# Second graph layer: one-hot sums in three bf16 parts in place of fp32 products

## The chip, the cores and the metric

The kernel runs on one core of a Trainium2 chip, in one launch. The metric is the device time of one execution in microseconds. Eleven executions of the kernel before took 3299.36 to 3309.21 us, with a median of 3303.67 us. The engines are named as the profile names them: PE (TensorE, the matrix engine; PEld is its weight load), DVE (VectorE), ACT (ScalarE), POOL (GpSimd) and SP (SyncE).

## What is computed

The reference is two rounds of a graph network with a feed-forward block after each. There are 6250 nodes with 256 features and 106,250 edges, sorted by destination. The change lies in the graph step of the second round. It projects every node, squares, sums the squares over a node's incoming edges with the weight of each edge, takes the root, and projects again:

```python
h = jax.nn.relu(x @ Wp.T + bp)            # 6250 x 128
hp = h ** MU                              # MU = 2
msgs = edge_vals[:, None] * hp[src]       # one weighted row an edge
agg = jax.ops.segment_sum(msgs, dst, num_segments=N)
agg = agg ** (1.0 / MU)
return h @ W1.T + b1 + agg @ W2.T + b2
```

A layer norm and a mixture of four small experts with a shared network follow on every node.

## The kernel before

**Stages.** The kernel goes through the first graph layer, the first feed-forward block (with its attention over 131,072 edges) and then the last stage, which holds the second graph layer and the second feed-forward block together. Only the last stage is touched. It begins at about 2214 us of the 3304.

**Tiles and groups.** The edges lie in T1 = 831 tiles of 128, one edge a partition. Six tiles (G1) make a group, so there are 139 groups, the last one of three tiles. Since edges are sorted, the destinations of a tile lie within a window of NW = 96 nodes whose first node `first_node(t)` (L998) is known beforehand. The nodes lie in 49 blocks of 128, which are put together in `blocks` (L2456): ten of four, three of two, three of one.

**What one group passes through.** `fetch(k)` (L2682) gathers the 128-wide rows `hp[src]` of group k from memory, with one indirect DMA a tile (helper `gather`, L1184), issued by POOL, into a tile `hg` that has six buffers. `weights_of(k)` (L2687) makes, for each tile, a 128 x 96 fp32 matrix `eq` on DVE: each row has the edge's weight in the column of its destination and zeros elsewhere (L2691). Its input `lanes`, the numbers 0 to 95, lies in PSUM (`px`, L2507), and the column of destinations and weights in SBUF. `add_up(k)` (L2696) multiplies `hg` (as weights of the array) with `eq` (streamed) on PE in fp32 and adds up in a PSUM tile of the node block (L2714); each fp32 product is two matmul records and two weight loads in the profile. A tile whose window crosses the border of a block takes two products.

**What runs beside it.** When a block's last edge is in, `roots` (L2722) takes the square root on ACT, `end_of2` (L2521) projects and normalises, `gates2` (L2551) picks experts on DVE, and `experts2` (L2609) runs the networks on PE, ACT and DVE and writes the output rows. These are generators: `advance_two` and `advance(routes, 1)` let them go a step further at set places, two of them inside `add_up`.

**The order.** The loop at L2762 runs once a group: issue the gathers of group k + 4 (`AHEAD`), make `eq` of k + 1, add up k, advance the rest; from k = 104 (`LATE`) the rest is advanced more often. This is the order of the source. The framework under the kernel places each engine's instructions anew, by an estimate of its own of when each can run, and keeps only the dependences. Within an engine the built program then runs strictly in that placed order. `pin` (L41) fixes only SP's queue here. A gather into a buffer of `hg` waits until the last reader of that buffer's former contents has ended: fetch k + 6 waits for the PE products of k.

```python
while k < len(groups2) or complete or coming or ends or routes or layers:
    if k + AHEAD < len(groups2):
        fetch(k + AHEAD)
    if k + 1 < len(groups2):
        weights_of(k + 1)
    if k < len(groups2):
        add_up(k)
    else:
        advance_two()
```

Of the kernel before, what the change touches and what calls it, by code (L numbers as in the profile page):

```python
# [9 lines left out]
F32 = mybir.dt.float32  # L10
I32 = mybir.dt.int32
AF = mybir.ActivationFunctionType
OP = mybir.AluOpType
# [4 lines left out]
P = 128  # L18
# [896 lines left out]
BF16 = mybir.dt.bfloat16  # L915
# [3 lines left out]
def kernel(ctx: ExitStack, tc: tile.TileContext, a: dict, out: bass.AP):  # L919
# [30 lines left out]
    G1 = 6  # L950
# [13 lines left out]
    PD = a["L1_gnn_Wp_T"].shape[1]  # L964
# [33 lines left out]
    def first_node(t):  # L998
        return min(max((t * NS >> 8) - 44, 0), NP - NW)

    with ExitStack() as fast:
# [41 lines left out]
        start = edges.tile([P, T], I32, name="start")  # L1043
# [7 lines left out]
        if T1 > C1:  # L1051
            V.memset(flat.bitcast(I32)[:, C1:T1], 2**24)
            n = E1 - C1 * P
# [394 lines left out]
        with ExitStack() as layer:  # L1448
# [73 lines left out]
            with (  # L1522
# [11 lines left out]
                for t0, t1 in parts0:  # L1534
                    b = t0 // TB
# [5 lines left out]
                    for i in range(t1 - t0):  # L1541
                        t = t0 + i
# [30 lines left out]
            with (  # L1573
# [10 lines left out]
                equals, et, ph, sums = {}, {}, {}, {}  # L1584
# [15 lines left out]
                def rows_of(q):  # L1600
                    return ring[q % len(ring)]
# [33 lines left out]
                def add_up(q):  # L1635

                    w, g = groups1[q]
                    if g == 0:
                        sums[w] = pse.tile([P, WS], F32, name="pe")
                    eq = equals.pop(q)  # L1640
                    if w == T - 1:
                        for j in range(G1):
                            TE.matmul(
                                sums[w], eq[j][0], rows_of(q)[:, j, 0:WS],
                                start=g == 0 and j == 0, stop=g == NG - 1 and j == G1 - 1,
                            )
# [133 lines left out]
        sums = attention.enter_context(tc.tile_pool(name="sums", bufs=1))  # L1780
# [4 lines left out]
        ew = weights.tile([P, T1], F32, name="ew")  # L1785
# [90 lines left out]
        def advance(queue, n):  # L1876
            for _ in range(n):
                if queue and next(queue[0], queue) is queue:
                    queue.pop(0)
# [3 lines left out]
        with (  # L1883
# [17 lines left out]
            for at in range(0, NM * P, D):  # L1901
                n = min(D, NM * P - at)
# [32 lines left out]
            def fetch(g):  # L1935
                got[g] = wk.tile([P, G, GW], F32, name="sg", bufs=4)
                for j in range(len(tiles2[g])):
                    gather(got[g][:, j, :], gat_dram, src2[:, g * G + j : g * G + j + 1])
# [287 lines left out]
            def node_values(ws):  # L2226
# [55 lines left out]
            src_of, dst_of = (  # L2282
                v.rearrange("p w a t -> p (w a t)")[:, 0:T1] for v in (src1, dst1)
            )
# [157 lines left out]
            k = NA + 5  # L2442
# [15 lines left out]
        with (  # L2458
# [49 lines left out]
            lanes = px[:, 0:P]  # L2508
# [100 lines left out]
            def experts2(b):  # L2609
# [66 lines left out]
            groups2 = [range(t, min(t + G1, T1)) for t in range(0, T1, G1)]  # L2676
            src_of, dst_of = (
                v.rearrange("p w a t -> p (w a t)")[:, 0:T1] for v in (src1, dst1)
            )
            gathered, equals, sums = {}, {}, {}  # L2680

            def fetch(k):  # L2682
                gathered[k] = wk.tile([P, G1, PD], F32, name="hg", bufs=6)
# [2 lines left out]

            def weights_of(k):  # L2687

                equals[k] = wk.tile([P, G1, NW], F32, name="eq", bufs=3)
                for j, t in enumerate(groups2[k]):  # L2690
                    V.tensor_scalar(  # L2691
                        equals[k][:, j, :], lanes[:, 0:NW], dst_of[:, t : t + 1],
                        ew[:, t : t + 1], op0=OP.is_equal, op1=OP.mult,
                    )

            def add_up(k):  # L2696

                hg, eq = gathered.pop(k), equals.pop(k)
                for j, t in enumerate(groups2[k]):
                    n0 = first_node(t)  # L2700
                    if j == 2 or j == 4:
                        advance_two()
                    for b, (t0, n) in enumerate(blocks):
                        lo, hi = max(n0, t0 * P), min(n0 + NW, (t0 + n) * P)
                        if lo >= hi:
                            continue
                        if b not in sums:
                            sums[b] = pse.tile([P, BT * P], F32, name="pe")
                            TE.matmul(
                                sums[b][:, 0 : n * P], ident, nothing[:, 0 : n * P],  # L2710
                                start=True, stop=False,
                            )
                        after = first_node(t + 1) if t + 1 < T1 else NP
                        TE.matmul(  # L2714
                            sums[b][:, lo - t0 * P : hi - t0 * P], hg[:, j, :],
                            eq[:, j, lo - n0 : hi - n0], start=False,
                            stop=after >= (t0 + n) * P,
                        )
                        if after >= (t0 + n) * P:
                            complete.append(b)  # L2720

# [9 lines left out]
            def advance_two():  # L2731

                if layers:
                    some = layers.pop(0)
                    if next(some, some) is not some:
                        layers.insert(min(1, len(layers)), some)
# [21 lines left out]
            for k in range(AHEAD):  # L2758
                fetch(k)
            weights_of(0)  # L2760
            k = 0
            while k < len(groups2) or complete or coming or ends or routes or layers:  # L2762
                if k + AHEAD < len(groups2):
                    fetch(k + AHEAD)
                if k + 1 < len(groups2):
                    weights_of(k + 1)
                if k < len(groups2):
                    add_up(k)
                else:
                    advance_two()  # L2770
                step_ends(k)
                if k >= LATE:
                    advance_two()
                    advance(routes, 1)
                while complete:
                    coming += roots(complete.pop(0))
                advance_two()
                advance(routes, 1)
                if k >= LATE:
                    advance_two()  # L2780
                    step_ends(k)
                k += 1


        with (
# [6 lines left out]
            n = wk.tile([P, NB + 7], F32, name="n")  # L2792
# [4 lines left out]
            for i in range(2):  # L2797
                k = NB + 1 + 2 * i
# [55 lines left out]
```

## Time and profile before

| what | us |
|---|---|
| median of 11 runs | 3303.67 |
| the profiled execution, its own time | 3305.74 |
| its span, first to last instruction | 3304.0 |
| PE busy over the span | 2996.0 (91%) |
| DVE busy | 2187.1 (66%) |
| ACT busy | 1183.3 (36%) |
| POOL busy | 2273.9 (69%) |
| mean granted PE clock | 0.894 |
| first gather of the last stage begins | 2214.30 |
| its last gather begins | 3250.49 |
| last product of L2714 begins | 3257.6 |

Busy time does not count register, branch, semaphore and DMA-issuing instructions, except that a POOL gather (`DMA_INDIRECT`) shows as an instruction of its own, the time in which POOL makes the descriptors. A group's row gives its line, engine, operation, output and inputs, count, then busy time, mean ns of one, and the idle time of the engine just before. A granted clock below 1 means that the PE ran slower than its full speed in that stretch.

### The profile page before, as it was taken

The page shows a single profiled execution, that of the slowest core. Times are in us where ns is not written, and L with a number is a line of the kernel's source. Part 1 is how long each engine was busy: PE and PEld are TensorE (multiplying, and loading weights), DVE is VectorE, ACT ScalarE, POOL GpSimd, SP SyncE. Part 2 cuts the span into 40 slices and gives each one's busy share as a digit, 9 for nine tenths or more (in the row PEclk, how much of TensorE's full clock was granted, in tenths as well). Part 3 has the DMA queues.
Part 4 walks back from the last instruction along what each step waited for, and adds up shares of the span by engine and source line. Part 5 has one row for each costly group of instructions (what it writes and reads, how often), then busy time and mean ns, then how long its engine had stood idle before and what let it go on. Part 6 is the DMA issues. An engine that isn't in the chain of part 4 may idle for free.

```text
span 3304.0 us, 59987 instructions
## 1 busy us (share of the span) xinstructions
PE 2996.0 (91%) x18517; PEld 2355.0 (71%) x18517; DVE 2187.1 (66%) x6516; ACT 1183.3 (36%) x2200; POOL 2273.9 (69%) x2720
## 2 busy tenths in 40 slices
PE   6899999999999989999999999956788889889997
PEld 5677777777777767888888888844566666656675
DVE  6687887888777765877686869862344444444464
ACT  5122222223222323456666668840112112112234
POOL 1576777777777774777776677427777777777772
PEclk9999999999999999999999999965577777777798
DMA  5898898989998873445454536532222222222221
GB/s 178 192 197 188 203 205 194 202 198 211 205 207 201 194 173 103 111 109 134 106 146 108 140 96 153 132 104 53 53 59 60 60 60 53 65 60 59 60 66 30
DMA packets 704935, 423.34 MB, mean 128 GB/s; under 512 B 538699, under 2 KB 647303, under 8 KB 704604
## 3 DMA queue, kind: packets, MB, share of 16 engines
q1 hardware_dynamic: 422972, 201.12, 23.3%
q0 software_dynamic: 88512, 171.58, 22.9%
q10 hardware_dynamic: 193120, 46.69, 7.0%
q8 instruction: 150, 2.46, 0.3%
q14 instruction: 181, 1.48, 0.2%
HBM read 382.75 MB, written 42.50 MB: 129 GB/s over the span
## 4 chain that ended last, share of the span: by engine, by line
PE 48%; POOL 18%; DMA 13%; issue 11%; DVE 7%; SPq 2%; ACT 2%; ACTq 0%; DVEq 0%; POOLq 0%
PE ph L1170 26%; POOL hg L1184 15%; PE py L1170 9%; DMA ea<-in_edge_attr_dram 6%; PE pe L1650 4%; PE pt L1170 3%; DMA hg<-hp_dram,src 3%; POOL sg L1184 2%; PE pe L2714 2%; DVE et L1613 2%; DMA sg<-gat_dram,src 1%; PE po L2032 1%; PE pa L1955 1%; DMA h<-y_dram,src 1%; DMA rb<-low_dram 1%
## 5 line engine op out<-in xcount | busy, mean ns | idle before, releaser
L1184 POOL DMA_INDIRECT h<-y_dram,src x882 | 859.7, 975 | 368.0 <-issue 200.5
L1184 POOL DMA_INDIRECT hg<-hp_dram,src x831 | 784.2, 944 | 280.4 <-issue 236.7
L1170 PE MATMUL ph<-w1b,et 128*128 128x256 f32 x3528 | 831.0, 387 | 15.6 <-DVE et L1613 8.8
L1184 POOL DMA_INDIRECT sg<-gat_dram,src x612 | 610.0, 997 | 273.6 <-issue 165.3
L1170 PEld LDWEIGHTS ph<-w1b,et 128*128 128x128 f32 x3528 | 658.7, 191 | 163.3 <-issue 79.5
L2714 PEld LDWEIGHTS pe<-eq,hg 128*128 128x128 f32 x2036 | 395.2, 259 | 298.7 <-issue 144.8
L2714 PE MATMUL pe<-eq,hg 128*128 128x96 f32 (+15 forms) x2036 | 449.6, 352 | 152.5 <-DMA hg<-hp_dram,src 128.5
L2691 DVE TENSOR_SCALAR eq<-px,dst,ew 128x96 f32<-128x96 f32 x831 | 262.3, 368 | 243.7 <-PE pe L2714 145.0
L1170 PE MATMUL py<-w,hh 128*128 128x256 f32 x1568 | 399.7, 393 | 13.7 <-ACT hh L1833 12.3
L1170 PE MATMUL ph<-b_all,w 128*128 128x256 f32 (+1 forms) x1600 | 401.6, 388 | 0.9 <-ACT hh L1833 0.9
L1632 ACT ACTIVATE h<-h 128x1536 f32<-128x1536 f32 x147 | 218.3, 1485 | 505.8 <-DVE h L1631 229.5
L1631 DVE TENSOR_TENSOR h<-ph,h 128x1536 f32<-128x1536 f32 x147 | 258.2, 1756 | 169.1 <-PE ph L1170 118.1
L1170 PEld LDWEIGHTS py<-w,hh 128*128 128x128 f32 x1568 | 282.4, 192 | 52.0 <-ACT hh L1833 17.6
L1170 PEld LDWEIGHTS ph<-b_all,w 128*128 128x128 f32 x1600 | 283.5, 191 | 30.7 <-ACT hh L1833 1.5
L1613 DVE STREAM_TRANSPOSE et<-ea 128x1536 f32<-128x1536 f32 x147 | 260.7, 1773 | 14.8 <-DMA ea<-in_edge_attr_dram 9.8
L1833 ACT ACTIVATE hh<-ph,b 128x256 f32<-128x256 f32 (+1 forms) x400 | 166.8, 466 | 126.1 <-PE ph L1170 106.3
L2010 DVE TENSOR_SCALAR E<-nodes,bits 128x256 bf16<-128x256 bf16 (+5 forms) x612 | 187.7, 347 | 35.2 <-PE po L2032 34.2
L1650 PE MATMUL pe<-h,eq 128*32 128x257 f32 x2496 | 180.6, 394 | 0.0
L1833 ACT ACT_TABLE_LOAD x102 | 130.9, 1283 | 22.5 <-PE ph L1170 12.6
L1165 ACT ACTIVATE b_all<-pt 128x256 f32<-128x256 f32 x147 | 53.9, 377 | 216.1 <-PE pt L1164 213.9
L1170 PE MATMUL py<-ew,g 65*128 65x256 f32 x392 | 128.3, 456 | 1.0 <-DVE miss L2799 1.0
L1650 PEld LDWEIGHTS pe<-h,eq 128*32 128x32 f32 x2496 | 72.5, 111 | 69.5 <-issue 35.1
(358 smaller groups left out, 3931.9 us busy)
## 6 DMA issues: line engine op xcount, KB each, us to landing
ea<-in_edge_attr_dram SPq DMA_DIRECT2D x784, 64.0 KB
ea<-in_edge_attr_dram ACTq DMA_DIRECT2D x392, 64.0 KB
w<-in_L_ffn_W_dram SPq DMA_DIRECT2D x48, 512.0 KB
y<-ys SPq DMA_DIRECT2D x96, 256.0 KB
rb<-low_dram SPq DMA_DIRECT2D x84, 256.0 KB
ea<-in_edge_attr_dram ACTq DMA_DIRECT2D x196, 96.0 KB
ea<-in_edge_attr_dram SPq DMA_DIRECT2D x196, 96.0 KB
h<-y_dram,src POOLq DMA_INDIRECT x882
```

The lines of the kernel that those rows point to most:

```text
L1165: SC.activation(dst, pt.rearrange("p c k -> p (c k)"), AF.Copy)
L1170: TE.matmul(dst, lhs(c), rhs(c), start=c == 0, stop=c == n - 1)
L1184: GP.indirect_dma_start(out=dst, out_offset=None, in_=table[0:NP, :], in_offset=IndirectOffsetOnAxis(ap=idx, axis=0), **more,)
L1613: V.transpose(et[q].rearrange("p c m k -> p m c k"), ahead.pop(q).rearrange("p m (c k) -> p m c k", c=2),)
L1631: V.tensor_add(h, ph.pop(q), h)
L1632: SC.activation(h, h, AF.Relu)
L1650: TE.matmul(sums[w][b * Q : (b + 1) * Q, :], some[:, (b - lo) * Q : (b - lo + 1) * Q], rows_of(q)[:, j, 0:WS], start=(g, b, j) in begin, s ...
L1833: SC.activation(hidden[u][:, f, :n, :], ph[:, f - f0, :n, :], AF.Gelu, bias=b1[:, e, f : f + 1],)
L1955: TE.matmul(pas[g][:, j, 0 : n * H], rows[g][:, j, :], part[:, i, b0 : b0 + n, :].rearrange("p t h -> p (t h)"), start=i == 0, stop=i == 2,)
L2010: V.tensor_scalar(Es[g, j][:, 0:n, :].rearrange("p b k -> p (b k)"), nodes16[:, 0 : n * P], bits.bitcast(F32)[:, g * G + j : g * G + j + 1 ...
L2691: V.tensor_scalar(equals[k][:, j, :], lanes[:, 0:NW], dst_of[:, t : t + 1], ew[:, t : t + 1], op0=OP.is_equal, op1=OP.mult,)
L2714: TE.matmul(sums[b][:, lo - t0 * P : hi - t0 * P], hg[:, j, :], eq[:, j, lo - n0 : hi - n0], start=False, stop=after >= (t0 + n) * P,)
```

## The change

The weight no longer goes into the one-hot matrix, but into the gathered rows. The one-hot matrix is then exact in bf16, and one DVE instruction makes it for a whole group. The weighted fp32 rows are split in three bf16 parts whose sum is the fp32 value: the first part is the row rounded to bf16, the second the rounded rest, the third the rest of that. The sum takes three bf16 products in place of one fp32 product. A group now has, on DVE, one `is_equal` (576 elements wide), one multiplication (`weighted`), and two subtractions (`less`, `least`), 768 wide each; on ACT two copies to bf16. The parts lie in a new tile `hp3` with three buffers; `eq` turns bf16. The source calls `weights_of` and `less` for k + 1, `weighted` for k + 2, and `least` for k + 1 after `add_up(k)`; the `else` with `advance_two` now belongs to the test of k + 1, so it runs once more, in the last group. What frees a buffer of `hg` is now the DVE subtraction of `least`.

```diff
             def weights_of(k):
 
-                equals[k] = wk.tile([P, G1, NW], F32, name="eq", bufs=3)
-                for j, t in enumerate(groups2[k]):
-                    V.tensor_scalar(
-                        equals[k][:, j, :], lanes[:, 0:NW], dst_of[:, t : t + 1],
-                        ew[:, t : t + 1], op0=OP.is_equal, op1=OP.mult,
-                    )
+                n = len(groups2[k])
+                at = slice(groups2[k][0], groups2[k][0] + n)
+                equals[k] = wk.tile([P, G1, NW], BF16, name="eq", bufs=3)
+                V.tensor_tensor(
+                    equals[k][:, 0:n, :], lanes[:, None, 0:NW].to_broadcast([P, n, NW]),
+                    dst_of[:, at].unsqueeze(2).to_broadcast([P, n, NW]), op=OP.is_equal,
+                )
+
+            def weighted(k):
+
+                n = len(groups2[k])
+                at = slice(groups2[k][0], groups2[k][0] + n)
+                hg = gathered[k][:, 0:n, :]
+                V.tensor_mul(hg, hg, ew[:, at].unsqueeze(2).to_broadcast([P, n, PD]))
+                split[k] = wk.tile([P, 3, G1, PD], BF16, name="hp3", bufs=3)
+                SC.activation(split[k][:, 0, 0:n, :], hg, AF.Copy)
+
+            def less(k):
+
+                n = len(groups2[k])
+                hg = gathered[k][:, 0:n, :]
+                V.tensor_sub(hg, hg, split[k][:, 0, 0:n, :])
+                SC.activation(split[k][:, 1, 0:n, :], hg, AF.Copy)
+
+            def least(k):
+
+                n = len(groups2[k])
+                V.tensor_sub(
+                    split[k][:, 2, 0:n, :], gathered.pop(k)[:, 0:n, :], split[k][:, 1, 0:n, :]
+                )
...
-                        TE.matmul(
-                            sums[b][:, lo - t0 * P : hi - t0 * P], hg[:, j, :],
-                            eq[:, j, lo - n0 : hi - n0], start=False,
-                            stop=after >= (t0 + n) * P,
-                        )
+                        for i in range(3):
+                            TE.matmul(
+                                sums[b][:, lo - t0 * P : hi - t0 * P], parts[:, i, j, :],
+                                eq[:, j, lo - n0 : hi - n0], start=False,
+                                stop=i == 2 and after >= (t0 + n) * P,
+                            )
...
             weights_of(0)
+            weighted(0)
+            less(0)
+            weighted(1)
+            least(0)
...
                 if k + 1 < len(groups2):
                     weights_of(k + 1)
+                    less(k + 1)
+                if k + 2 < len(groups2):
+                    weighted(k + 2)
                 if k < len(groups2):
                     add_up(k)
+                if k + 1 < len(groups2):
+                    least(k + 1)
                 else:
                     advance_two()
```

More of the change, by code (lines that the diff above doesn't have):

```diff
@@ L2679 @@
             )
-            gathered, equals, sums = {}, {}, {}
+            gathered, equals, split, sums = {}, {}, {}, {}
             def fetch(k):
@@ L2687, in weights_of @@
             def weights_of(k):
-                equals[k] = wk.tile([P, G1, NW], F32, name="eq", bufs=3)
-                for j, t in enumerate(groups2[k]):
-                    V.tensor_scalar(
-                        equals[k][:, j, :], lanes[:, 0:NW], dst_of[:, t : t + 1],
-                        ew[:, t : t + 1], op0=OP.is_equal, op1=OP.mult,
-                    )
+                n = len(groups2[k])
[22 more added lines that the diff above has]
+                )
             def add_up(k):
-                hg, eq = gathered.pop(k), equals.pop(k)
+                parts, eq = split.pop(k), equals.pop(k)
                 for j, t in enumerate(groups2[k]):
```

## The prediction

> **What bounds the last stage now.** I read the groups of the page first, then the table by stage, then the order in time. The groups that the change touches:
>
> ```profile
> L1184 POOL DMA_INDIRECT hg<-hp_dram,src x831 | 784.2, 944 | 280.4 <-issue 236.7
> L2714 PE MATMUL pe<-eq,hg 128*128 128x96 f32 (+15 forms) x2036 | 449.6, 352 | 152.5 <-DMA hg<-hp_dram,src 128.5
> L2691 DVE TENSOR_SCALAR eq<-px,dst,ew 128x96 f32<-128x96 f32 x831 | 262.3, 368 | 243.7 <-PE pe L2714 145.0
> ```
>
> The PE products wait mostly for gathers. The table by stage (columns: busy time and count of PE, PEld, DVE, ACT, POOL, then granted clock, DMA share, GB/s) says who sets the pace:
>
> ```profile
> 2600.00:2700.00 100.00, 84.45 (x317) 61.97 (x316) 41.51 (x152) 16.17 (x30) 75.57 (x81) 0.74 0.23 58
> 3100.00:3200.00 100.00, 97.28 (x462) 75.67 (x461) 53.27 (x214) 34.63 (x67) 75.63 (x81) 0.85 0.25 66
> 3253.10:3304.00 50.90, 30.02 (x178) 23.12 (x177) 23.24 (x113) 20.27 (x51) 0.00 (x0) 0.84 0.05 15
> ```
>
> POOL makes the same 81 gathers in each 100 us, whether PE is 84% or 97% busy. A gather takes 0.944 us and the next starts 0.30 us later: 1.247 us each. 830 x 1.247 = 1035 us, and first and last start lie 3250.49 - 2214.30 = 1036 us apart. So POOL's gathers bound the stage without a gap, and a faster PE buys nothing before 3250; behind the last gather stand 53.5 us of tail, where PE is 30 us busy. The chain of waits gives the landing:
>
> ```profile
> 2618.77 2.52 DMA hg<-hp_dram,src
> 2621.30 0.14 issue
> 2621.43 0.43 PE pe L2714 x2
> ```
>
> The gather issued at 2618.77 can be used 2.66 us later.
>
> **The change, part by part.** *PE.* Goes: 2036 fp32 records, 449.6 us. Comes: 1018 x 3 = 3054 bf16 products. The nearest row is the attention's 128x61 bf16 group, 2090 in 99.4 us at clock 1.0 (L2032): 0.048 us each, so about 0.075 for 96 columns. That is some 230 us, 220 less. All of it lies beside POOL: worth nothing while POOL sets the pace.
>
> *ACT.* Two copies of 768 a group. L1632's 1536 take 1.485 us, L1997's 160 take 0.34; between them 0.85. 278 x 0.85 = 236 us on an engine that is idle for three quarters of the stage: nothing.
>
> *DVE.* Goes 831 x 0.368 (262.3 us busy). Comes a group: `is_equal` on 576, and three operations on 768. Rows: 256 wide 0.42 (L2530), 512 wide 0.685 (L1849), 1536 wide 1.756 (L1631), so 1.046 ns an element: 0.75 and 3 x 0.95, 3.6 us in a group that lasts 7.48. With 1.9 us of the rest DVE is 73% full: not the bound by volume.
>
> *What these operations do to POOL.* This is the first price. Every DVE operation that runs during the stage's gathers today has an input in PSUM or a single tensor input, and the gathers take 940 to 957 ns. The three new 768-wide ones read two tensors in SBUF. The attention stage has such operations (order in time; start, duration):
>
> ```profile
> 1332.28 0.68 DVE L2051 TENSOR_TENSOR b<-lane,low 128x512 bf16<-128x512 f32 x1
> 1332.38 1.40 POOL L1184 DMA_INDIRECT sg<-gat_dram,src  x1 [0.30 <-issue]
> ...
> 1439.89 0.69 DVE L1849 TENSOR_TENSOR ys<-py,b 128x512 f32<-128x512 f32 x1
> 1439.93 0.94 POOL L1184 DMA_INDIRECT sg<-gat_dram,src  x1 [0.30 <-issue]
> ```
>
> L2051 has both inputs in SBUF; it covers the gather's start, and the gather ends at 1333.78, 0.82 us after L2051's end (1332.96). L1849, with one input in PSUM, covers a start as well and the gather keeps its 0.94. I went through all cases from 1270 to 2165 us: of gathers whose start was covered by L2051, L1999, L2002 or L2257 (two SBUF inputs, begun at least 0.04 us earlier, ended at least 0.16 later), 49 of 49 were longer, each by what the operation still had to run less 0.13 us (median deviation 0.01). Of those covered by L1849 or L2043 (one in PSUM), 0 of 34; by L2691, 0 of 27. Operations begun after a gather's start did nothing to it. So 0.95 us at a random moment meets a start with what is left: the delay averages 0.82 x 0.82 / 2 / 1.247 = 0.27 us. `weighted` is not at a random moment: it waits for a landing, 2.66 us behind a start, the next starts come at 2.49 and 3.74, and it ends at about 3.65: free. `less` and `least` fall anywhere: 0.54 a group. Bounds: nothing, if gathers of this table differ; 42 us if DVE has little else, for then `least` runs behind `weighted` and `is_equal` at 4.47 to 5.42, over the start at 4.99, and costs 0.30 x 139, with `less` free behind it; 0.81 x 139 = 113 us with all three at random.
>
> The Trainium skill, "SBUF — State Buffer", section "Who interferes with whom", speaks against this: a tensor_tensor with both inputs in SBUF takes only the read interface shared with GpSimd, a probe saw it not stall DMA, and it infers that descriptor generation needs the write interface. By it this term is 0 and the sum 3380. The 49 cases decide for me.
>
> *The order.* This is the second price. I compared the order in which the two built programs put their instructions on each engine. POOL's order is the same. On DVE, the placement believes in faster gathers than the trace shows, and puts `weighted` far ahead. Counting `least` behind `weighted(k)`: 100 of 139 stand at most three groups ahead, 21 four, 15 five, three (114, 119, 129) six. `weighted(k)` waits for group k's landing and everything behind it on DVE waits too. Two things follow.
>
> First, the gather ring. Gathers of k + 1 need the buffer that `least(k - 5)` frees. Where `weighted(k)` stands six ahead, that `least` is queued behind it: POOL idles for the landing (2.66), `weighted`, `less`, an ACT copy and `least` (3.7), some 6.5 us; 3 x 6.5 = 20. At five ahead POOL has one group in hand (7.48 us), and DVE has `is_equal`, `less` and `least` with a dozen small operations that wait for PE: I take 1 us each, 15. Sum 35; bounds 0 and 18 x 6.5 = 117. For the 40 groups in such bunches I count no contention beside it, so contention is 99 x 0.54 = 53 us.
>
> Second, the end. `weighted(138)`, which waits for the very last landing, stands on DVE ahead of `is_equal(131)`. So PE can't begin `add_up(131)` before that. From there to the last product PE has 222 bf16 products (17 us) and about 27 us of expert and projection products (counted in the order, by their rows of 3195 to 3304, as 14 of 128x256 at 0.59 and so on): 44 us after 4.1 us of landing and DVE, so the last product is 48 us after the last gather. Before it was 7.1. What follows (46 us of the last block's chain) stays. Tail +41; +10 if much of that PE work comes earlier than I read, +60 if DVE and PE wait for each other.
>
> **Sum.** 53 + 35 + 41 = 129 us on 3305.74: 3435. The median of the runs lies 2 us below the profiled one: **3433 us**.
>
> **Rivals.**
> - *The relief of PE counts* (faster). In the tail PE was 7 us behind the last gather; with bf16 it keeps up and the end comes 7 us earlier: 3297. It decides if two SBUF inputs do not hold these gathers and PE's last groups are not held by `weighted(138)`. For it: 97% PE before the end. Against: the constant 81 gathers, the 49 cases, the order. 3%.
> - *All of it is hidden*: gathers keep their 0.944 and the bunches resolve, 3304, within 0.2% of before (about what a measurement of this kernel can tell from no change). 3%.
> - *No contention, only the order*: 35 + 41, 3380. Decided by gathers of 0.94 in the stage. 10%.
> - *DVE or PE becomes the bound.* The granted clock was 0.50 from 2214 to 2300 with PE 57% busy; if a PE with less to do falls there, the 61 us of PE work from `add_up(131)` to the end that is not bf16 becomes 61 x 0.84 / 0.50 = 102, and each bunch lengthens: with all three operations at random (+60) and this (+41), 3534. For it: operations on DVE that wait for PE in the bunches. Against: a busier PE was granted 0.74 to 0.85. 12%.
> - Forecast with its own bounds: 72%. Each tile does get one `is_equal` a group and three products in the built program, so the change does what it says.
>
> **Chances and range.** Low: 42 + 0 + 10 over 3304 gives 3356; high: 113 + 60 of the ring's 117 + 45 of the tail's 60, since the three will hardly be at their worst together, gives 3522. With the rival at 3380 inside, little more than 2 in 10 lies out. Faster by over 0.2%: 3%; within: 3%; slower: 94%.
>
> **What would show it.** Right: gathers of `hg` with a mean near 1.01 us and single ones up to 1.8, stretched ones ending 0.82 us after a 768-wide operation; POOL idle for 5 us or so before a gather, put down to DVE, in a few places near 40%, 75% and after 80% of the groups; the stage's gathers spanning some 1125 us; the tail near 95. Wrong: gathers at 0.944 throughout; last gather to end at 50 us; a long DVE queue with POOL's gap at 0.30 everywhere.

## The result, and the profile after

The changed kernel took 3455.48 us (median of 8 runs, 3453.18 to 3458.32) where the kernel before took 3303.19 in the same comparison (31 runs, 3296.89 to 3309.80): 1.046 times as long, 95% interval 1.0452 to 1.0470. The forecast was 3433 with a range of 3356 to 3522. The profiled execution has a span of 3451.0 us; before it was 3304.0.

The groups of the page of the kernel after. As before, the columns are line, engine, operation, output and inputs, count, then busy time, mean ns of one, and the idle time of the engine just before with what ended it:

```profile
L1184 POOL DMA_INDIRECT hg<-hp_dram,src x831 | 854.1, 1028 | 318.6 <-issue 236.1
...
L2739 PE MATMUL pe<-eq,hp 128*128 128x96 bf16 (+15 forms) x3054 | 220.8, 232 | 295.5 <-DVE eq L2692 147.0
L2702 DVE TENSOR_TENSOR hg<-hg,ew 128x768 f32<-128x768 f32 (+1 forms) x139 | 132.6, 954 | 470.1 <-DMA hg<-hp_dram,src 465.7
...
L2704 ACT ACTIVATE hp<-hg 128x768 bf16<-128x768 f32 (+1 forms) x139 | 116.3, 837 | 276.8 <-DVE hg L2702 134.7
...
L2716 DVE TENSOR_TENSOR hp<-hg,hp 128x768 bf16<-128x768 f32 (+1 forms) x139 | 131.5, 946 | 14.0 <-ACT hp L2711 13.7
```

The products take 220.8 us in place of 449.6, and they now wait mostly for `eq` on DVE, no longer for gathers. The gathers are the group that grew: 944 to 1028 ns each. They are the same 831 transfers with the same code.

The table by stage of the kernel after (stretch; busy time and count of PE, PEld, DVE, ACT and POOL; granted clock, DMA share, GB/s):

```profile
2600.00:2700.00 100.00, 76.81 (x506) 49.21 (x507) 67.84 (x147) 44.20 (x66) 78.06 (x73) 0.80 0.22 59
3100.00:3200.00 100.00, 56.26 (x357) 37.09 (x358) 51.80 (x122) 33.83 (x51) 63.92 (x64) 0.73 0.18 48
3350.00:3451.00 101.00, 67.63 (x484) 52.98 (x483) 51.41 (x194) 42.94 (x92) 3.96 (x4) 0.75 0.05 14
```

The 81 gathers in each 100 us have become 73 at 2600 and 64 at 3100. At 2600 POOL is busier than before (78.06 against 75.57) and makes fewer gathers, so each takes longer. At 3100 it is less busy (63.92), so it waits. Behind the last gather stand about 100 us with PE, DVE and ACT all at work.

I took the span apart at three marks: the first gather of the last stage, its last gather, and the end. "Stretching" is what the 831 gathers took together over the 784.2 us of the kernel before, "gaps" the sum of POOL's idle time before a gather over the usual 0.305 us.

| us | before | after | difference |
|---|---|---|---|
| first gather of the stage | 2214.3 | 2210.0 | -4 |
| first to last gather | 1036.2 | 1143.4 | +107 (stretching 70, gaps 38, by sums that overshoot by 1) |
| last gather to the end | 53.5 | 97.6 | +44 |
| span | 3304.0 | 3451.0 | +147 |

**Stretching.** The trace of the kernel after in order of time (start, duration, engine and line), one gather of many:

```profile
2528.38 0.96 DVE L2716 TENSOR_TENSOR hp<-hg,hp 128x768 bf16<-128x768 f32 x1 [2.14 <-ACT hp L2711]
2528.60 1.56 POOL L1184 DMA_INDIRECT hg<-hp_dram,src  x1 [0.30 <-issue]
```

`least` (L2716) runs from 2528.38 to 2529.34. The gather starts inside it and ends at 2530.16, which is 0.82 us after `least`. All 149 gathers over 0.97 us end 0.82 us after one of the three new operations: 59 after `less` (L2710, 26.0 us together), 72 after `least` (36.9 us), 18 after `weighted` (L2702, 7.1 us). In nearly all cases that is the operation which ran when the gather started. Here it was the next one:

```profile
2800.23 0.94 DVE L2702 TENSOR_TENSOR hg<-hg,ew 128x768 f32<-128x768 f32 x1
...
2800.58 2.27 POOL L1184 DMA_INDIRECT hg<-hp_dram,src  x1 [0.30 <-issue]
...
2801.10 0.95 DVE L2716 TENSOR_TENSOR hp<-hg,hp 128x768 bf16<-128x768 f32 x1
```

The gather starts inside `weighted`, `least` follows without a break, and the gather ends some 0.8 us after `least`.

**Gaps.** Seven idle times of POOL are over 0.8 us, 40 us together, of which 38 are over the usual 0.305: before group 36 (3.80), 73 (0.83), 115 (7.14), 116 (4.73), 120 (5.93), 130 (11.54) and 135 (6.02). The trace of POOL, the first gather of groups 115 and 130 (in brackets the idle time before and what ended it):

```profile
3140.54 0.94 POOL L1184 DMA_INDIRECT hg<-hp_dram,src  x1 [7.14 <-DVE hp L2716]
...
3280.91 0.94 POOL L1184 DMA_INDIRECT hg<-hp_dram,src  x1 [11.54 <-DVE ln_rs L2539]
```

The first is put down to `least`, the second to a small operation of DVE that ended just after a `least` of 3279.69 to 3280.64, which freed the buffer.

**The end.** The chain of waits of the kernel after (start, length, what):

```profile
3353.38 3.96 DMA hg<-hp_dram,src
...
3358.74 2.19 PE pe L2739 x32
```

and the trace in order of time just behind it:

```profile
3357.46 0.56 DVE L2702 TENSOR_TENSOR hg<-hg,ew 128x384 f32<-128x384 f32 x1 [3.33 <-DMA hg<-hp_dram,src]
3357.94 0.75 DVE L2692 TENSOR_TENSOR eq<-px,dst 128x576 bf16<-128x576 f32 x1
...
3358.74 0.45 PE L2739 MATMUL pe<-eq,hp 128*128 128x16 bf16 x7 [15.38 <-DVE eq L2692]
```

`weighted(138)` waits for the last landing, `is_equal(131)` stands behind it on DVE, and PE, which had waited 15.38 us for this, only then begins the eight last groups. The last run of products begins at 3400.91, 47.5 us behind the last gather (7 before). From there the end takes 50 us (46 before).

### The profile page after: what moved, and what is told of

The parts are those of the page before. It is cut to its first block, busy times and chain, and to the rows that moved or that the text cites. A ratio compares the mean times of both kernels' runs of the same rounds, so it can differ in the third digit from the quotient of the medians.

```text
span 3451.0 us, 62307 instructions
## 1 busy us (share of the span) xinstructions
PE 2804.7 (81%) x19535; PEld 2158.9 (63%) x19535; DVE 2376.3 (69%) x6241; ACT 1410.1 (41%) x2488; POOL 2342.3 (68%) x2720
## 5 line engine op out<-in xcount | busy, mean ns | idle before, releaser
L1184 POOL DMA_INDIRECT hg<-hp_dram,src x831 | 854.1, 1028 | 318.6 <-issue 236.1
L2739 PE MATMUL pe<-eq,hp 128*128 128x96 bf16 (+15 forms) x3054 | 220.8, 232 | 295.5 <-DVE eq L2692 147.0
L2702 DVE TENSOR_TENSOR hg<-hg,ew 128x768 f32<-128x768 f32 (+1 forms) x139 | 132.6, 954 | 470.1 <-DMA hg<-hp_dram,src 465.7
L2739 PEld LDWEIGHTS <-hp 128*128 128x128 bf16 x3054 | 193.4, 119 | 413.6 <-issue 227.4
L2704 ACT ACTIVATE hp<-hg 128x768 bf16<-128x768 f32 (+1 forms) x139 | 116.3, 837 | 276.8 <-DVE hg L2702 134.7
L2711 ACT ACTIVATE hp<-hg 128x768 bf16<-128x768 f32 (+1 forms) x139 | 116.1, 837 | 140.6 <-DVE hg L2710 139.9
L2716 DVE TENSOR_TENSOR hp<-hg,hp 128x768 bf16<-128x768 f32 (+1 forms) x139 | 131.5, 946 | 14.0 <-ACT hp L2711 13.7
```

What stands on the lines that cost most here:

```text
L1184: GP.indirect_dma_start(out=dst, out_offset=None, in_=table[0:NP, :], in_offset=IndirectOffsetOnAxis(ap=idx, axis=0), **more,)
L2702: V.tensor_mul(hg, hg, ew[:, at].unsqueeze(2).to_broadcast([P, n, PD]))
L2704: SC.activation(split[k][:, 0, 0:n, :], hg, AF.Copy)
L2716: V.tensor_sub(split[k][:, 2, 0:n, :], gathered.pop(k)[:, 0:n, :], split[k][:, 1, 0:n, :])
L2739: TE.matmul(sums[b][:, lo - t0 * P : hi - t0 * P], parts[:, i, j, :], eq[:, j, lo - n0 : hi - n0], start=False, stop=i == 2 and after >= ( ...
```

## Experiments

The theory has two parts. First, contention: an operation of DVE with two tensor inputs in SBUF holds back a gather whose start it covers, and POOL's gathers set the pace of the stage. Second, the order: `weighted` placed far ahead of `least` and `is_equal` makes POOL wait for buffers and keeps the last products back. The main rivals: gathers slow down because DVE is busier or the memory is, whatever the operands; and PE's relief, or a lower PE clock, decides at the end. Ten kernels were run. In the table "last product" is the start of the last run of sum products behind the last gather; all figures but the ratios are of the profiled execution, in us.

| kernel | ratio to before (95%) | span | stretching | gaps | tail | last product |
|---|---|---|---|---|---|---|
| before | | 3304.0 | | | 53.5 | 7 |
| after | 1.0452 to 1.0470 | 3451.0 | 70 | 38 | 97.6 | 48 |
| d1_two_sbuf | 1.0351 to 1.0386 | 3423.3 | 85 | 0 | 65 | 19 |
| d2_one_psum | 1.0111 to 1.0145 | 3340.5 | 0 | 0 | 89 | 44 |
| a1_one_psum | 1.0039 to 1.0072 | 3325.5 | 3 | 0 | 72 | 21 |
| a2_in_turn | 1.0285 to 1.0319 | 3398.7 | 92 | 0 | 67 | 18 |
| b1_products | 0.9978 to 0.9997 | 3290.4 | 0 | 0 | 48 | 3 |
| a5_thirds | 1.0213 to 1.0250 | 3371.3 | 58 | 2 | 69 | 20 |
| a6_turn_thirds | 1.0181 to 1.0222 | 3358.2 | 50 | 0 | 69 | 20 |
| a7_order_alone | 1.0325 to 1.0363 | 3410.4 | 1 | 68 | 97 | 53 |
| a8_end_in_turn | 1.0393 to 1.0448 | 3430.2 | 75 | 32 | 82 | 32 |
| a9_rest_in_turn | 1.0418 to 1.0453 | 3450.6 | 87 | 23 | 98 | 48 |

**Two inputs in SBUF, or one (d1_two_sbuf, d2_one_psum).** Three more operations a group stand beside the unchanged kernel before; only the second input differs.

```diff
+            extra_a = wp.tile([P, G1, PD], F32, name="extra_a")
+            extra_b = wp.tile([P, G1, PD], F32, name="extra_b")
...
                         ew[:, t : t + 1], op0=OP.is_equal, op1=OP.mult,
                     )
+                    if j % 2 == 0 and len(groups2[k]) == G1:
+                        V.tensor_tensor(extra_a, extra_a, extra_b, op=OP.max)
```

In d2 `extra_b` in the last line is `lanes[:, None, 0:PD].to_broadcast([P, G1, PD])`, which lies in PSUM.

> The kernel before, with three added VectorE operations of 768 elements in each group that nothing else uses; both inputs lie in SBUF. Theory (an operation with two SBUF inputs that covers a gather's start holds it back for the rest of its run): they stand between the one-hot operations, at no fixed phase, so about 0.27 us each and 0.8 us a group, mean gather 1.05 to 1.10 us in place of 0.944, last gather 80 to 130 us later, time 3385 to 3435. Rival (the gathers suffer from something else in the change, as the engines' load or the waits): gathers stay at 0.944 and the time at 3303 to 3315, as VectorE has room for 2.9 us more in a group.

> The same three added operations of 768 elements a group, but the second input is the row of numbers in PSUM. Same VectorE time, one SBUF input. Theory: gathers stay at 0.944 us, time 3300 to 3315. Rival (VectorE's load or its order slows the stage): the same time as with two SBUF inputs.

The gathers of d1 and then of d2, from the view of the tile `hg` (count: minimum, median, maximum in ns, first and last start):

```profile
L1184 POOL DMA_INDIRECT hg<-hp_dram,src x831: 941/947/1729, 2236.5 to 3358.2; - x167
```

```profile
L1184 POOL DMA_INDIRECT hg<-hp_dram,src x831: 940/944/1453, 2215.2 to 3251.8; - x167
```

From first to last gather d1 takes 1121.7 us and d2 1036.6; in the kernel before it was 1036.2. The operations last as long in both (949 and 942 ns) and DVE is about as busy (73.6 and 79.7 us of 100 at 2600), so it is the operand and not the load. (The time of d1, 3425 us, lies in its expected range, but 22 us of its loss are a later first gather, which the theory does not explain.) Nor is it PSUM that spares a gather: `bn_stats` (L2532) reads one SBUF tensor and nothing in PSUM, and of the 13 gathers of the kernel before whose start it covers none took over 0.947 us. It is the second input in SBUF. The trace of d1 and then of d2, one gather each:

```profile
2604.03 0.96 DVE L2701 TENSOR_TENSOR extra_a<-extra_a,extra_b 128x768 f32<-128x768 f32 x1
...
2604.22 1.59 POOL L1184 DMA_INDIRECT hg<-hp_dram,src  x1 [0.31 <-issue]
```

```profile
2605.67 0.94 DVE L2701 TENSOR_TENSOR extra_a<-extra_a,px 128x768 f32<-128x768 f32 x1
...
2606.44 0.94 POOL L1184 DMA_INDIRECT hg<-hp_dram,src  x1 [0.30 <-issue]
```

In d1 the gather ends at 2605.81, 0.82 us after the operation's end at 2604.99. In d2 the operation covers the start from 2605.67 to 2606.61 and the gather keeps its 0.94.

The time of d2 missed its expectation, by 28 us or more: the tail grew by 35. The stretch of d2 from 2600 to 2700, and its tail:

```profile
2600.00:2700.00 100.00, 91.11 (x322) 68.67 (x322) 79.72 (x210) 19.49 (x32) 75.48 (x80) 0.65 0.23 58
3252.00:3340.00 88.00, 64.42 (x332) 51.83 (x332) 48.21 (x191) 35.12 (x78) 0.74 (x1) 0.79 0.04 11
```

DVE is 80% busy while POOL makes its undisturbed 80 gathers. Group by group, I compared the start of the first `eq` with the start of the group's last gather. Up to group 42 `eq` is up to 19 us ahead, from group 48 to 108 the two are within 8 us of each other, in group 114 `eq` is 12 us behind and in group 138 it is 36 behind. So DVE falls behind the gathers in the last quarter, and the backlog is paid in the tail. In group 138 of the kernel before `eq` is 2 us behind, and in d1 14, where the gathers come later. That is a cost which the theory did not have: a DVE with little room pays at the end. Whether the volume makes this or the placement, which differs between d1 and d2 as well, was not parted.

**The change without the contention, and without the order (a1_one_psum, a2_in_turn).** In a1 the three operations of the kernel after read a row of PSUM in place of the second SBUF input; the placement then changes as well, and puts `weighted` at most two groups ahead.

```diff
-                V.tensor_mul(hg, hg, ew[:, at].unsqueeze(2).to_broadcast([P, n, PD]))
+                V.tensor_tensor(hg, hg, lanes[:, None, 0:PD].to_broadcast([P, n, PD]), op=OP.max)
...
-                V.tensor_sub(hg, hg, split[k][:, 0, 0:n, :])
+                V.tensor_tensor(hg, hg, lanes[:, None, 0:PD].to_broadcast([P, n, PD]), op=OP.max)
```

(and `least` likewise). In a2 the operations are those of the kernel after, and a dependence holds each of `is_equal`, `weighted`, `less` and `least` behind the one that precedes it in the source:

```diff
+            def in_turn():
+                i = tc.nc.cur_bb.bb.instructions[-1]
+                if last_split:
+                    tc.add_manual_dep(i, last_split.pop(), ..., reason="keep_in_program_order")
+                last_split.append(i.name)
...
                 V.tensor_mul(hg, hg, ew[:, at].unsqueeze(2).to_broadcast([P, n, PD]))
+                in_turn()
```

> The changed kernel, with the multiplication and both subtractions replaced by a maximum with the row of numbers in PSUM: same widths, same outputs and waits, one SBUF input (weighting and splitting are left out, so the sums are other numbers). In the built order weighted stands at most two groups ahead of least throughout, which the changed kernel's does not. Theory: gathers at 0.944 us, no gap on GpSimd, end of the gathers near 3248, PE two groups behind at the end, tail 50 to 60: 3295 to 3312. Rival (the wait chain of the split itself, or PE and VectorE, set the pace): 3380 or more, gaps on GpSimd.

> The changed kernel with nothing left out; only the placed order of the four VectorE operations of the groups is held to that of the source, so that weighted stands two groups ahead of least throughout. Theory (order costs 40 us of gaps before gathers and 44 us of tail; contention 70 us): gaps gone, tail 52 to 62, mean gather still 1.00 to 1.05 us: 3360 to 3385. Rival A (the order is not the cause of gaps and tail): 3440 to 3460. Rival B (waits alone, no contention): 3300 to 3312.

In a1 gathers and gaps are all but those of the kernel before (one gather is longer by 0.94 us, the median is 947 ns in place of 944), and most of the loss is gone: 1.0055 in place of 1.0461. This run takes away both parts at once, so it does not tell them apart. Its one long gather is a test of the theory by itself. The stage has a single other operation with two inputs in SBUF, L2497 (one partition, 1024 wide), and here it covers that gather's start:

```profile
2239.42 1.22 DVE L2497 TENSOR_TENSOR ew<-ew,sb 1x1024 f32<-1x1024 f32 x1
...
2239.58 1.88 POOL L1184 DMA_INDIRECT hg<-hp_dram,src  x1 [0.30 <-issue]
```

The gather ends 0.82 us after it. The one long gather of d2 and the one of a7 end 0.82 us after L2497 too. In the kernel before L2497 held none: one gather starts 0.16 us before it, the next 0.12 us before its end. The time lies 9 us or more over the expectation, and the loss is nearly all tail, 72 against 53.5. In a2 the gaps are gone and the tail fell by 30 us, as expected, but the stretching rose from 70 to 92, and the time is 3402 where 3360 to 3385 was expected. The view of the tile `hg` of a2:

```profile
L1184 POOL DMA_INDIRECT hg<-hp_dram,src x831: 940/944/1828, 2203.7 to 3331.5; - x167
```

First to last gather: 1127.8 us, 92 more than before, with `least` 48, `less` 38 and `weighted` 7. So the order of the kernel after goes with some 22 us less contention than that of the source.

**The order alone (a7_order_alone).** The reverse of a2: the operations of a1 that do not disturb gathers, written out and held in exactly the order of the kernel after.

```diff
+            ORDER = ("e0 e1 e2 W0 l0 W1 z0 l1 e3 W2 z1 l2 W3 e4 z2 l3 W4 e5 z3 l4 "
...
+                "z132 W136 l133 W137 z133 W138 e131 e132 e133 e134 l134 z134 ... e138 ").split()
```

(e is `is_equal`, W `weighted`, l `less`, z `least`; each is issued in this order, with the dependence of a2.) DVE's other operations stand up to some 30 places from where they stand in the kernel after.

> The order of after without the contention: the four VectorE operations of all groups are held to exactly the order that they have in the kernel after (weighted up to six groups ahead, weighted(138) ahead of is_equal(131)), but the three 768-wide operations read one input from PSUM (the row of lane numbers, with a maximum). It leaves out the weighting and the splitting. Theory (the order's price stands by itself): gathers at 0.944, gaps of some 40 us before groups 115, 116, 120, 130 and 135 and near 36, a tail of 90 to 98, together 3375 to 3395. Rival (gaps and tail come only because gathers are late and VectorE is held up by the contention): no gap over 1 us or a tail near 72, 3310 to 3330, as with one PSUM input in the tidy order.

The gathers, and one gap, the first gather of group 130 (view of the tile `hg`, then POOL in order of time):

```profile
L1184 POOL DMA_INDIRECT hg<-hp_dram,src x831: 938/944/1820, 2208.1 to 3312.9; - x167
```

```profile
3231.99 0.94 POOL L1184 DMA_INDIRECT hg<-hp_dram,src  x1 [15.66 <-issue]
```

With every gather but one at 0.94 the gaps are still there, before the groups where the kernel after has them: 36 (3.3), 115 (13.3), 116 (5.2), 120 (7.2), 130 (15.7) and 135 (15.5), with 37, 71, 105, 122 and 131 beside them. The tail is 97. The order's price therefore stands by itself; the rival, that lateness of the gathers makes gaps and tail, falls. The gaps are larger than in the kernel after (68 against 38), and the expectation of 3375 to 3395 was 15 us short.

The two halves do not add up. Over the stretch from first to last gather contention alone (a2) costs 92 us and the order alone (a7) 69; together, in the kernel after, 107 and not 160. So each hides part of the other. That a late POOL finds its buffers free, and that a POOL which waits for a buffer meets fewer operations, would explain it; no run shows this gather by gather.

**Where the order costs (a8_end_in_turn, a9_rest_in_turn).** The dependence of a2 for the last groups only, or for all but the last:

```diff
             def in_turn(k):
+                if not (k >= 131):     # a8; in a9: k < 126
+                    return
```

> The kernel after with the four VectorE operations held to the order of the source for groups from 131 on only; up to weighted(131) the built order is that of after, instruction by instruction of the four. Nothing is left out. Theory (the tail comes from weighted(138) ahead of is_equal(131), and the gaps before groups 36, 115, 116, 120 and 130 come from the order before them): the gap before 135 goes (6 us), the other gaps stay at some 34 us, the tail falls from 98 to 65 to 75: 3412 to 3430. Rival (PE is behind at the end for other reasons, the clock or the bunches before): the tail stays over 88 and the time over 3440.

> The reverse: the four operations held to the order of the source for groups below 126 only; from there the built order is that of after, with weighted(138) ahead of is_equal(131). Nothing is left out. Theory: the gaps before 36, 115, 116 and 120 go, those near 130 and 135 stay (10 to 18 us), contention is that of the run held in turn (some 85 to 92), the tail stays at 90 to 98: 3435 to 3455. Rival (late gathers let VectorE and PE catch up, so that the end's order costs little): tail under 75, 3400 to 3420.

In a8 the gap before 135 is gone and the five before it stand where they stood (4.8, 7.1, 4.7, 5.8, 11.3), as expected. The tail fell only by half of what was expected, to 82. That is above the expectation's 65 to 75 and under the rival's 88, so `weighted(138)` ahead of `is_equal(131)` explains some 16 of the 44 us. I take a further 15 (82 against the 67 of a2) for backlog from the bunch at groups 126 to 130, which a8 keeps and a2 does not have; no run parted this from other causes. The last 14 (67 against 53.5) are there even in the order of the source. In a9 the end is that of the kernel after, PE again waiting (PE of a9 in order of time):

```profile
3340.75 1.22 PE L1170 MATMUL py<-ew,g 65*128 65x256 f32 x2
3358.40 1.87 PE L2761 MATMUL pe<-eq,hp 128*128 128x16 bf16 x28 [16.43 <-DVE eq L2709]
```

Tail 98 and contention 87, as expected; the gaps are 23 where 10 to 18 was expected, since the built order bunches at groups 127 to 131 instead. Its rival, late gathers making the end's order cheap, falls. Mending the order of nine tenths of the groups took only some 8 us from the time (1.0436 against 1.0461) and nothing from the profiled span: the gaps lost 15 us, and the stretching gained 17.

**Shorter operations (a5_thirds, a6_turn_thirds).** Each of the three operations is cut in pieces of two tiles; a6 also has the dependence of a2, on each piece.

```diff
-                V.tensor_sub(hg, hg, split[k][:, 0, 0:n, :])
+                for c in range(0, n, 2):
+                    d = min(c + 2, n)
+                    V.tensor_sub(hg[:, c:d, :], hg[:, c:d, :], split[k][:, 0, c:d, :])
```

> The kernel after with each of the three 768-wide operations cut in three pieces of two tiles (256 wide, 0.42 us each by the row of 256). Nothing is left out. Theory (a gather waits only for the operation that covers its start, for what is left of it less 0.13): a piece at a random moment costs 0.29 x 0.29 / 2 / 1.247 = 0.034, nine pieces 0.30 us a group where three whole ones cost 0.81, so the 70 of after (92 held in turn) become 26 to 34. The pieces also change the placement: in the built order only one weighted stands five groups ahead of least, ten four, and weighted(138) behind the products' is_equal of 137, so the gaps fall to under 10 and the tail to 65 to 75. Together 3340 to 3360. Rival (the pieces run back to back and hold a gather like one long operation): gathers stretched by 70 or more, 3385 to 3400.

> Both mends at once: the kernel after with the three operations cut in pieces of two tiles, and is_equal, weighted, less and least of all groups held to the order of the source on VectorE. Nothing is left out. Theory: contention 34 in place of the 92 of the run held in turn without pieces, gaps under 5, tail 65 to 75: 3340 to 3355. If the pieces hold gathers like whole operations: 3395 to 3410, as without them.

Both came out between theory and rival: 3373 and 3360 us, with a stretching of 58 and 50 where the theory said 26 to 34 and the rival 70 or more. Three pieces back to back show as one row of 1.09 us in the trace, a piece beginning every 0.33. DVE and POOL of a6, in order of time:

```profile
2666.02 1.09 DVE L2744 TENSOR_TENSOR hp<-hg,hp 128x256 bf16<-128x256 f32 x3
...
2666.89 1.03 POOL L1184 DMA_INDIRECT hg<-hp_dram,src  x1 [0.30 <-issue]
```

The gather starts in the third piece and waits only for that one: it ends at 2667.92, 0.81 after 2667.11. Of the gathers of a6 that start well within a row of two or three pieces (0.05 us after its begin, 0.16 before its end), 196 of 221 end 0.82 us after the piece that covered them. Those held by less than 0.32 us add up to 34 us, the theory's figure. The other 16 us are 18 gathers held by 0.32 to 1.8 us, through the piece that covers them and one or more of those behind it. In a5 the same split is 33 and 25. Of the 18 gathers over 1.5 us in a6, 16 were released by the end of a piece of `weighted`; why a gather sometimes does not get in between two pieces is not settled. a6, at 1.020, is the best of the versions that compute the whole thing, but still slower than the kernel before.

**PE's part alone (b1_products).** The kernel before with one bf16 `is_equal` a group and three bf16 products:

```diff
-                            sums[b][:, lo - t0 * P : hi - t0 * P], hg[:, j, :],
-                            eq[:, j, lo - n0 : hi - n0], start=False,
...
+                        upper = hg[:, j, :].bitcast(BF16).rearrange("p (d h) -> p d h", h=2)
+                        for i in range(3):
+                            TE.matmul(
+                                sums[b][:, lo - t0 * P : hi - t0 * P], upper[:, :, 1],
+                                eq[:, j, lo - n0 : hi - n0], start=False,
```

> The kernel before with the PE part of the change alone: one bf16 is_equal a group, and three bf16 products a tile in place of the fp32 one, reading the upper halves of the gathered fp32 rows as they lie. It leaves out the weight of each edge and the split in parts; nothing else works on the gathered rows. Theory (POOL's gathers bound the stage, PE's relief buys nothing before the last gather): 3293 to 3308, gathers at 0.944, first to last gather 1036 us as before, PE's busy time over the stage some 220 us lower. Rival (the relief of PE counts): first to last gather shorter than 1030, or a time below 3285. Rival (a PE with less to do is granted a low clock, and the tail becomes longer): over 3315, with the granted clock of the last 50 us below 0.7.

The page's group of its products, and its gathers from the view of the tile `hg`:

```profile
L2717 PE MATMUL pe<-eq,hg 128*128 128x96 bf16 (+15 forms) x3054 | 275.7, 229 | 292.9 <-DMA hg<-hp_dram,src 284.8
```

```profile
L1184 POOL DMA_INDIRECT hg<-hp_dram,src x831: 940/944/957, 2205.9 to 3241.9; - x167
```

PE's products lose 174 us (some 220 were expected), and first to last gather is 1036.0 us, as before. What the relief is worth is the tail, 48.5 in place of 53.5, and a ratio of 0.9988: 4 us of 3304. The rival of a low clock falls: from 3241 us to the end it was granted 0.85. So PE was not the bound, and this is also why no version of the split can win much here: with nothing else added the gain was these 4 us, and every operation that the split adds has to cost less.

## Why the prediction was right

**PE, ACT and DVE's volume.** 3054 products at 0.075 us were to take 230 us; 220.8. That row was scaled by width alone, from a stage at clock 1.0, while this one ran at 0.50 to 0.80, and with other orders the same products took 219 to 253, so the closeness is partly luck. The copies on ACT 0.85, 0.837. On DVE `is_equal` 0.75 and the three operations 0.95: 0.745 and 0.946 to 0.954. That all the PE relief lies beside POOL holds: b1.

**Contention, predicted 53, measured 70.** The mechanism is as predicted, with the same constants: a gather whose start is covered is longer by the rest of the operation less 0.13. In the kernel after, a2 and d1, 515 of 515 gathers covered by one of the three operations with two SBUF inputs (begun at least 0.05 us earlier, ending at least 0.16 later) were longer, and their median is within 0.01 us of that rule; in d2, a1 and a7, with one input in PSUM, none of 597 was longer by over 0.02 us. Counted with the margins of the prediction, the trace of the kernel before gives 50 of 50 for the operations with two SBUF inputs, 0 of 58 for L1849 and L2043 and 0 of 118 for L2691: other counts than mine, the same answer. That no operation beside the stage's gathers had two tensor inputs in SBUF was not quite so: L2497 has, once.

Against it I had set the Trainium skill, "SBUF — State Buffer", section "Who interferes with whom": a probe there did not see a tensor_tensor stall DMA, and the page infers that descriptor generation needs the write interface, which a tensor_tensor does not take. By that this term would be 0; for these gathers d1 against d2 decides otherwise, 85 us against 0.4 from first to last gather. I had left out the other half of the section: it also states that an operation of DVE with two SBUF inputs contends with a GpSimd instruction that reads SBUF. The measured contention fits that half if the gather counts as such an instruction, which no run here tests.

The 17 us that were missing are the bunches. I counted none for the 40 groups where `weighted` stands four or more ahead. Counting with each `weighted(k)` the gathers of group k + 1, these groups have 16 us of stretching in the kernel after, 0.43 each, and the others 53 us, 0.54 each, which is what I had for them. By operation the shares differ: I took 0.27 each for `less` and `least`; over all 139 groups they cost 0.19 and 0.27 in the kernel after, 0.27 and 0.35 in a2. And `weighted`, costed at nothing because it ends before the next start, costs 7 us: 18 gathers were held by it all the same.

**Gaps, predicted 35, measured 38.** The three places where the order puts `weighted` six ahead (114, 119, 129) gave the gaps before 115, 120 and 130: 7.1, 5.9 and 11.5, together 25 for the predicted 20. The gap before 116 (4.7) belongs to 114 too, since `least(110)`, which frees its buffer, also stands behind `weighted(114)`. The fifteen at five ahead were to cost 1 us each, 15; two of them, 34 and 133, gave the gaps before 36 and 135 (3.8 and 6.0), one of 0.8 follows the pair 67 and 68, and the others cost nothing. So the sum came near with the parts divided otherwise. a7 has them without any contention and a2 has none with it.

**Tail, predicted +41, measured +44.** The last product was to come 48 us behind the last gather; 47.5. The total was right, and the chain of it is in the trace, though its parts made up for each other: 5.4 us to the first product where I had 4.1, then 39 us of PE work for my 44 (12 of products where I had counted 17), and 3 of waits that I did not have. Moreover the experiments divide it otherwise than I did: `weighted(138)` ahead of `is_equal(131)` was to be the whole cause, and holding the end in order (a8) took back only 16 us. Some 14 stay even in the order of the source (a2; 18 in a1). That a group's rows now pass five more steps on DVE and ACT behind the landing, and that DVE is fuller, are likely causes; no run parted them. My sum hit the total because PE's work from group 131 on does stand behind that landing; once that wait is taken away, another one is there.

**The rivals.** PE's relief is worth 4 us (b1), measured with nothing else added. "Only the order" was priced at 3380; a7 measures 3410 for it, since gaps are larger when gathers are not late. "DVE or PE becomes the bound" did not happen in the kernel after: the granted clock was 0.75 in the tail and 0.66 to 0.80 in the stretches of 100 us from 2400 on. Something like it was seen in d2, where DVE at 80% ended 36 us behind. Of the 22 us by which the forecast lies low, 18 show in the profiled executions: contention 17, gaps 3 and tail 3, less the 4 by which the stage began earlier and 1 by which the sums overshoot. The other 4 come from the medians: the profiled execution of the kernel before lies 2 us above its median, that of the kernel after 2 us below.

## What to carry to other kernels

Before a faster engine is paid for with work on another, find out who sets the pace and what that work does to it: here the relief of the busiest engine (91%) was worth 4 us, and three operations on an engine with room cost 85 by their operands alone (d1 against d2). Where POOL issues gathers without a gap, look at the operands of everything that DVE runs beside them; with one input in PSUM the contention was gone, and with shorter pieces nearly half of it. And read the built order, not the source: an operation that waits for a landing and is placed ahead of the one that frees its buffers made gaps at the very groups that the order shows, and costs of this kind do not add up, so that mending one alone uncovers another.

## What was not expected of the hardware

- A gather is held by the operation that runs when it starts: of those where one of the three operations merely began later (by 0.05 us or more), 0 of 519 were longer (after, a2 and d1). But a gather that is held can stay held through the next such operation, where by the trace that one begins up to 0.09 us before the first has ended: 3 gathers in the kernel after, 7 in a2 and 20 of the 282 longer ones in a6. Most are released between the two even then, and what decides it is open. In d1, whose operations do not overlap in the trace, no gather was held by two.
- The granted clock does not follow PE's load in these runs. From 2600 to 2700 it was 0.74 with PE busy 84 us of 100 (before), 0.80 with 77 (after), 0.64 with 76 (b1), 0.61 with 69 (a2) and 0.65 with 91 (d2). What sets it stays open.
- The stage's first gather begins between 2202.8 and 2215.2 us in all runs but d1, where it begins at 2236.5. The prediction's sum had no term for this, and I have no explanation for those 22 us, which are a fifth of d1's loss.
